# Position bias of layer 0: two kinds of DMA change their issuing engine, and the softmax its step

## The chip, the cores and the metric

The program runs on one core of a Trainium2 chip. The metric is the device time of one execution in microseconds. Three executions of the kernel before took 3286.91, 3290.55 and 3295.93 us, so the median is 3290.55 us. A separate execution was recorded by the hardware profiler.

## What is computed

Four layers are chained; only the first matters here. It is an attention over an image of 32 x 32 positions, with 2 images and 8 heads each, so 16 heads in all. Every head has 1024 queries and 64 keys, whose places are sampled by learned offsets. To every score a bias is added, which a small network of three layers computes for each pair of a query and a key:

```python
pos = grid_q[:, :, None, :] - grid_kv[:, None, :, :]
bias = jnp.sign(pos) * jnp.log1p(jnp.abs(pos))
bias = jax.nn.relu(bias @ cpb_w1 + cpb_b1)          # 2 -> 128
bias = jax.nn.relu(bias @ cpb_w2 + cpb_b2)          # 128 -> 128
bias = (bias @ cpb_w3 + cpb_b3).reshape(b, GROUPS, H * W, Hd * Wd)
sim = jnp.einsum('bhid,bhjd->bhij', qh, kh) + bias
attn = jax.nn.softmax(sim, axis=-1)
out = jnp.einsum('bhij,bhjd->bhid', attn, vh)
```

All arithmetic is in fp32. The bias network over 16 x 1024 x 64 pairs is the bulk of layer 0.

## The kernel before

**Steps.** `layer0` walks through 256 steps `(u, o, half)`: `u` is the head (0 to 15), `o` a group of 8 keys (0 to 7), and `half` one of its two sets of 4 keys. The text writes (4,1) for `o` = 4, `half` = 1. The order on PE, ScalarE (ACT), VectorE (DVE) and GpSimd (POOL) is written out by hand under `manual_schedule`; each engine runs its own list in that order. SyncE (SP) is not in that set; its DMA issues are placed by the framework, and SP runs them one after the other as well.

**A step.** `first_hidden` (called one step ahead) makes the first hidden layer of 4 keys on DVE (line 741), four instructions of 128 x 1024, from a table `tx` (x part) and a row `bank` (y part, line 726). `second_hidden` multiplies by the second weights, one quarter `q` of the 128 outputs at a time: 16 matmuls of line 768 give one tile `hp` in PSUM, of which there are three. ACT takes the ReLU of each quarter from PSUM (line 782; q0 is also multiplied by a sign, lines 785 and 787). In some steps of `u` > 0 (`late`, `early`) DVE takes one quarter instead (lines 777 and 780). The four quarters are then added: q0 into q1 by an accumulating DMA that POOL issues (line 792), q2 into q3 by POOL (line 796), and both sums by POOL in the next step (`join`, line 799). Quarter tiles `h2_0` have two buffers, so a ReLU of q0 needs the DMA of line 792 of two steps before to have landed.

**Folding.** The tile of q3 holds both halves of a group; three such tiles exist (`two_tiles`). `refold` halves its partitions by accumulating DMAs (lines 802, 824, 827), and two copies on SP (line 834, `sum<-h`) gather the rest into one of two tiles `sum` of the head. These copies come two groups after their group, and the tile is free for the group after that. Three `sum` tiles rotate over the heads, so the copies of group 1 into the second `sum` tile of head `u` write where the first `sum` tile of head `u-1` still lies.

**Summed rows.** While head `u` is in its groups 1 to 4, the two `sum` tiles of head `u-1` are finished: ACT multiplies by a sign (line 222), POOL issues two accumulating DMAs (lines 839 and 841, `keys_rows`), and two copies of 64 KB put the result into the tile `rows` (line 845, on SP). The `refolds` list says at which step each piece is issued: the copies of the first tile at the end of step (3,0), those of the second at the end of step (4,0). At (5,0) `attend` is queued: it adds `rows` to the scores and takes the softmax on DVE and ACT, one piece per step (lines 890 to 940).

**Logarithms.** `table` works for two groups at a time. In the steps that prepare odd groups it loads the next 16 keys' logarithms (`lb<-logs`, 512 KB, broadcast to 128 partitions, line 678 through `send`, line 493) into one of two buffers, and puts a POOL instruction right behind it in POOL's order that turns their x part into `tx` (line 681). `send` issues on SP, behind the last gathering copy recorded in `self.gathered`, which lines 831, 834 and 845 set. The load for groups 6 and 7 is thus issued in the step (4,1), behind the row copies of the second `sum` tile in SP's order.

**Other front work.** The offsets and sampled keys of later pairs of heads run as generators, one piece per step (`front`), and yield to `attend` (`after`).

Of the kernel before, what the change touches and what calls it, by code (L numbers as in the profile page):

```python
# [11 lines left out]
F32 = mybir.dt.float32  # L12
# [6 lines left out]
P = 128  # L19
B, C, H, W = 2, 512, 32, 32  # L20
# [3 lines left out]
HF = 512  # L24
# [33 lines left out]
class Net:  # L58
# [40 lines left out]
    def layer0(self):  # L99


        nc, io = self.nc, self.io
        with ExitStack() as ctx:
# [45 lines left out]
            with self.tc.manual_schedule(engines=engines):  # L149
                pairs = [{} for _ in range(BP)]  # L150
# [26 lines left out]
                tables = {}  # L177
# [12 lines left out]
                for i, (u, o, half) in enumerate(quads):  # L190
                    self.half = half
                    if o == 2 and half == 1 and u % 2 == 0 and u // 2 + 1 < BP:
                        nxt = pairs[u // 2 + 1]
                        front += [self.offsets(nxt, u // 2 + 1, ps), self.sampled(nxt, u // 2 + 1, ps)]
                    h1 = ready
                    if i + 1 < len(quads):
                        if quads[i + 1][1:] == (7, 0) and u + 1 < 2 * BP:
                            self.advance(front, lambda: "logs" in pairs[(u + 1) // 2])
                        ready = self.first_hidden(*quads[i + 1], pairs, tables)
                    last_set = u == last and o >= 4  # L200
                    if half == 0:
                        if o == 0:
                            before, sums = sums, []
                        if o % 4 == 0:
                            group = []
                        if i + 2 < len(quads):
                            both = self.two_tiles(f"h2_{u}_{o}3")
                            group.append([both[:, 0, :], both[:, 1, :], both])
                        else:
                            group.append([self.four_rows(f"h2_{u}_{o}{n}3") for n in range(2)])  # L210
                        if o < 2:
                            sums.append(self.four_rows(f"sum{u}_{o}"))
                    self.second_hidden(i, u, o, half, h1, group[-1], i + 1 == len(quads), last_set)
                    if half == 1 and not last_set:
                        end = i + (3 if u == last else 4)
                        self.refolds.append((i + 2, end, end, self.refold(group[-1][2], sums[o % 2], o // 2, u == last)))
                    v = u - 1
                    if half == 1 and o in (1, 2) and 0 <= v < last - 1:
                        z = before[o - 1]
                        if o == 1:  # L220
                            rows = self.soft.tile([P, HF], F32, tag="pt", name=f"rows{v}")
                        nc.scalar.activation(z, z, AF.Copy, scale=self.last_sign)
                        self.refolds.append((i + 2, i + 4, i + 3, self.keys_rows(z, rows, o - 1)))
                    if half == 1 and o == 2 and v >= 0:
                        sims[v] = ps_s.tile([P, HF], F32, tag="sim", name=f"sim{v}")
                        if v == last - 1:
                            self.sum_product(sims[v], self.thrice, True, before)
                        self.advance(front, lambda: "v" in pairs[v // 2])
                        self.keys_queries(v, pairs[v // 2], sims[v], v < last - 1)
                    if v >= 0 and (o, half) == ((5, 0) if v < last - 1 else (2, 1)):  # L230
                        if v == 8:
                            self.advance(after, lambda: False)
                            att = [apool.tile([P, N], F32, tag=f"att{t}", name=f"att{v}_{t}") for t in range(CT)]
                        after.append(self.attend(v, pairs[v // 2], sims[v], att, ps, rows if v < last - 1 else None))
                        if v % 8 == 7:
                            after.append(self.projection(ps, att, ow, v // 8))
                    elif half == 1 and u == last and o == 5:
                        sims[u] = ps_s.tile([P, HF], F32, tag="sim", name=f"sim{u}")
                        self.sum_product(sims[u], self.twice[:, 16:48], True, sums)
                    elif half == 1 and u == last and o == 7:  # L240
                        self.sum_product(sims[u], self.folded[:, 8:40], False, [one[0] for one in group[:2]])
                    self.refold_more(i, True)
                    if not self.step(after):
                        self.step(front)
# [419 lines left out]
    def turn(self, m, bt, ps):  # L664
# [2 lines left out]
            self.nc.tensor.transpose(tr[:, n, :], m["xn"][:, n * P : (n + 1) * P], self.ident)  # L667
        return tr

    def table(self, u, o, pairs, tables):  # L670

        nc = self.nc
        def load(u, c):
            logs = pairs[u // 2]["logs"].rearrange("(a j c i) e -> a c j (i e)", a=2, j=2, c=4)[u % 2, c]
            got = self.lpool.tile([P, 2, 8, 2, W], F32, tag="logs", name=f"lb{u}{c}")
            self.send(got.rearrange("p j i d x -> p j (i d x)"), logs.unsqueeze(0).to_broadcast([P, 2, 16 * W]))
            x = self.tab.tile([P, 2, 8, W], F32, tag="x", name=f"tx{u}{c}")
            with self.behind(self.added):  # L680
                nc.gpsimd.tensor_scalar(  # L681
                    x, got[:, :, :, 0, :], self.col("cpb_w1", 0), self.col("cpb_b1"), ALU.mult, ALU.add
                )
            tables["next"] = got, x

        y = self.bank[:, 0:256].rearrange("p (i x) -> p i x", i=8)
        jj = o % 2
        if u == 0 and o < 2:


            if o == 0:
                tables["x"] = self.tab.tile([P, 2, 8, W], F32, tag="x", name="tx00")
            else:
                load(0, 1)
            mask = self.ident[:, 32 * jj : 32 * jj + 8]
            parts = []
            for d in range(2):
                at = self.fone.tile([P, 8, W], F32, tag=f"first{d}", name=f"first{o}{d}")
                nc.vector.tensor_tensor(
                    at,  # L700
                    pairs[0]["log"][:, d, :].unsqueeze(1).to_broadcast([P, 8, W]),
                    mask.unsqueeze(2).to_broadcast([P, 8, W]),
                    ALU.mult,
                )
                got = self.ps_h.tile([P, 8, W], F32, tag="ps", name=f"lb_ps{o}{d}")
                nc.tensor.matmul(
                    got.rearrange("p k x -> p (k x)"),
                    lhsT=self.all,
                    rhs=at.rearrange("p k x -> p (k x)"),
                    start=True,  # L710
                    stop=True,
                )
                parts.append(got)
            next(self.weights)
            x = tables["x"][:, jj, :, :]
            nc.scalar.activation(x, parts[0], AF.Identity, scale=self.col("cpb_w1", 0), bias=self.col("cpb_b1"))
            nc.vector.tensor_scalar(y, parts[1], self.col("cpb_w1", 1), None, ALU.mult)
            if o == 0:
                next(self.weights)
            return x, y  # L720
        if o % 2 == 0:
            tables["logs"], tables["x"] = tables.pop("next")
        elif u < 2 * BP - 1 or o < 7:

            load(*((u, o // 2 + 1) if o < 7 else (u + 1, 0)))
        nc.vector.tensor_scalar(y, tables["logs"][:, jj, :, 1, :], self.col("cpb_w1", 1), None, ALU.mult)
        return tables["x"][:, jj, :, :], y

    def first_hidden(self, u, o, half, pairs, tables):

        if half == 0:
            tables["xy"] = self.table(u, o, pairs, tables)
        x, y = tables["xy"]
        h1 = [self.hid.tile([P, 2, H, W], F32, tag="h1", name=f"h1_{u}_{o}{half}{r}") for r in range(2)]

# [100 lines left out]
    def keys_rows(self, z, to, jj):  # L836

        nc = self.nc
        nc.gpsimd.dma_start(z[0::2], z[1::2], accum_op=ALU.add)
        yield  # L840
        nc.gpsimd.dma_start(z[0::4], z[2::4], accum_op=ALU.add)
        yield
        for h in range(2):
            at = h * NJ + jj * 32
            self.gathered = nc.sync.dma_start(to[at : at + 32, :], z[0::4, h * HF : (h + 1) * HF])

    def sum_product(self, sim, lhsT, start, zs):

# [1348 lines left out]
```

## Time and profile before

| | |
|---|---|
| median of three executions | 3290.55 us |
| the profiled execution | 3290.0 us, span 3288.3 us, mean granted TensorE clock 0.995 |
| matmuls of line 768 | first at 22.9 us, last at 1966 us |
| PE busy | 3217.4 us, 98% of the span |
| DVE, ACT, POOL busy | 75%, 58%, 72% of the span |
| between 138 and 1853 us: PE, DVE, ACT, POOL busy | 1660, 1375, 1262, 1511 of 1715 us |
| loads of logarithms | 63, all on SP, median 6.3 us from issue to landing |
| copies into `rows` | 56, all on SP, median 2.6 us from issue to landing |

The profile's groups name a line, an engine, an operation and the tiles it writes and reads. A wait is idle time of an engine, put down to the event that ended it last; where that event was long over, another one released the engine. Heads 1 to 14 are the ones with the full pattern; their steps lie between 138 us (first matmul of head 1) and 1853 us (first matmul of head 15).

### The profile page before, as it was taken

To read this page: it belongs to the slowest core of one execution; us is meant where nothing else is said; L and a number is where in the kernel's file an instruction comes from. 1 tells how busy PE (TensorE), PEld (TensorE's weight loads), DVE (VectorE), ACT (ScalarE), POOL (GpSimd) and SP (SyncE) were. 2 spreads that over 40 slices of the span, in tenths; PEclk is the share of its full clock that TensorE was granted. 3 is DMA by queue.
4 is the path that set the end of the run, shared out by engine and by line. 5 is a ranking of instruction groups with operands and counts; after the bars stand their busy time and mean duration, and the time that the engine had idled before them with its cause. 6 is when DMAs were issued, how large, how long until landed. Compare 5 with 4: busy or idle time off the path is not lost.

```text
span 3288.3 us, 58784 instructions
## 1 busy us (share of the span) xinstructions
PE 3217.4 (98%) x23956; PEld 1210.3 (37%) x23956; DVE 2470.8 (75%) x2834; ACT 1905.2 (58%) x1985; POOL 2362.1 (72%) x1664
## 2 busy tenths in 40 slices
PE   9999999999999999999999999999999999999999
PEld 4333233233233323233333224444465533455333
DVE  7888878888878677888877775565565689855897
ACT  7877777777777577777777661111141466213662
POOL 7989888988988779989888974344153458534575
PEclk9999999999999999999999999999999999999999
DMA  6887787787787668787787763111000100000001
GB/s 169 161 173 158 147 174 154 154 169 152 152 163 154 129 136 165 148 172 158 146 171 157 152 151 137 39 44 47 0 1 1 39 1 1 15 1 13 1 1 53
DMA packets 96591, 341.92 MB, mean 104 GB/s; under 512 B 19888, under 2 KB 22064, under 8 KB 79216
## 3 DMA queue, kind: packets, MB, share of 16 engines
q0 software_dynamic: 56224, 244.88, 39.2%
q1 hardware_dynamic: 39072, 91.00, 9.0%
q8 instruction: 193, 3.16, 0.4%
q10 hardware_dynamic: 1008, 2.10, 0.2%
q14 instruction: 94, 0.77, 0.1%
HBM read 67.37 MB, written 4.46 MB: 22 GB/s over the span
## 4 chain that ended last, share of the span: by engine, by line
PE 63%; POOL 16%; DVE 9%; DMA 6%; issue 4%; ACT 1%; SPq 0%; DVEq 0%; POOLq 0%; ACTq 0%
PE hp L768 26%; POOL h L799 7%; PE s L1730 5%; PE o L1759 5%; DMA h<-h 3%; POOL h L796 3%; DVE h L741 3%; POOL h L792 2%; PE qk20P L1505 1%; PE qk30P L1505 1%; PE m_0P L1014 1%; PE m_7P L1014 1%; PE m_5P L1014 1%; PE m_4P L1014 1%; PE m_2P L1014 1%
## 5 line engine op out<-in xcount | busy, mean ns | idle before, releaser
L768 PE MATMUL hp<-h,w2s 128*32 128x512 f32 x16384 | 1816.7, 597 | 53.5 <-ACT h L782 47.9
L782 ACT ACTIVATE h<-hp,magb 128x1024 f32<-128x1024 f32 x950 | 1043.1, 1108 | 470.9 <-PE hp L768 306.5
L741 DVE CUSTOM_DVE_ANT_1 h<-tx,bank 128x1024 f32<-128x1024 f32 (+1 forms) x1028 | 1180.4, 1210 | 161.2 <-PE hp L768 121.7
L768 PEld LDWEIGHTS hp<-h,w2s 128*32 128x32 f32 x16384 | 559.0, 110 | 1276.8 <-issue 1069.1
L799 POOL TENSOR_TENSOR h<-h,h 128x1024 f32<-128x1024 f32 x254 | 750.5, 2955 | 14.0 <-DMA h<-h 11.8
L796 POOL TENSOR_TENSOR h<-h,h 128x1024 f32<-128x1024 f32 x209 | 661.9, 3167 | 5.1 <-ACT h L782 5.1
L792 POOL DMA_DIRECT2D h<-h x227 | 333.8, 1471 | 73.0 <-ACT h L782 64.6
L1734 ACT ACTIVATE e<-s 128x1024 f32<-128x1024 f32 x256 | 261.8, 1024 | 181.0 <-PE s L1730 175.1
L1759 PE MATMUL o<-e,v 64*64 64x512 f32 x2048 | 265.3, 589 | 2.1 <-DVE q L1798 2.1
L1730 PE MATMUL s<-q,k 64*64 64x512 f32 x2048 | 266.0, 591 | 0.0
L787 ACT ACTIVATE h<-h,flip 128x1024 f32<-128x1024 f32 x182 | 209.6, 1152 | 6.0
L1741 POOL TENSOR_TENSOR some<-some,e 128x1024 f32<-128x1024 f32 x64 | 167.6, 2619 | 26.6 <-ACT e L1734 24.1
L1739 POOL TENSOR_TENSOR some<-e,e 128x1024 f32<-128x1024 f32 x32 | 76.0, 2376 | 141.4 <-DVE sum L1748 102.4
L802 POOL DMA_DIRECT2D h<-h x127 | 173.1, 1363 | 6.1 <-issue 4.0
L824 POOL DMA_DIRECT2D h<-h x124 | 168.3, 1358 | 7.6 <-DMA h<-h 5.1
L827 POOL DMA_DIRECT2D h<-h x120 | 148.7, 1239 | 17.0 <-DMA h<-h 16.8
L681 POOL TENSOR_SCALAR tx<-lb,cols 128x512 f32<-128x512 f32 x63 | 78.4, 1245 | 108.9 <-DMA lb<-logs 72.5
L1746 DVE TENSOR_TENSOR sum<-sum,e 128x1024 f32<-128x1024 f32 x64 | 123.9, 1936 | 29.6 <-ACT e L1734 26.9
L984 POOL TENSOR_TENSOR mlp_w<-mlp_w 128x512 f32<-128x512 f32 x16 | 23.5, 1470 | 158.7 <-DMA mlp_w<-in_mlp_w 113.5
L1759 PEld LDWEIGHTS o<-e,v 64*64 64x64 f32 x2048 | 77.9, 133 | 144.9 <-issue 135.1
L1730 PEld LDWEIGHTS s<-q,k 64*64 64x64 f32 x2048 | 76.6, 133 | 133.2 <-issue 117.2
L777 DVE SCALAR_TENSOR_TENSOR h<-hp,under,h 128x1024 f32<-128x1024 f32 x46 | 59.0, 1283 | 79.1 <-ACT h L782 69.4
(595 smaller groups left out, 3583.5 us busy)
## 6 DMA issues: line engine op xcount, KB each, us to landing
h<-h POOLq DMA_DIRECT2D x354, 512.0 KB, 5.8
lb<-logs SPq DMA_DIRECT2D x63, 512.0 KB, 6.3
h<-h POOLq DMA_DIRECT2D x124, 256.0 KB, 4.3
mlp_w<-in_mlp_w SPq DMA_DIRECT2D x16, 1024.0 KB, 4.8
h<-h POOLq DMA_DIRECT2D x120, 128.0 KB, 3.8
sum<-h SPq DMA_DIRECT2D x240, 64.0 KB, 3.4
sum<-sum POOLq DMA_DIRECT2D x28, 256.0 KB, 5.0
x<-in_x SPq DMA_DIRECT2D x8, 512.0 KB, 7.9
```

Source lines behind the costliest of these rows:

```text
L741: self.nc.vector._custom_dve(TENSOR_ADD_SAT, out=h1[r][:, k, cut, :], in0=x[:, 4 * half + 2 * r + k, :].unsqueeze(1).to_broadcast([P, H // ...
L768: nc.tensor.matmul(hp[rows, cut], lhsT=self.l0w2[:, 32 * q : 32 * q + 32], rhs=h1[k][:, cut], start=True, stop=True)
L782: nc.scalar.activation(y, hp, AF.Relu, bias=self.magb[:, q, 0:1])
L787: nc.scalar.activation(y, y, AF.Copy, scale=self.flip)
L792: self.added = pool.dma_start(y, ys[0], accum_op=ALU.add)
L796: self.added = (vec if final else pool).tensor_tensor(y, y, ys[2], ALU.add)
L799: (vec if final else pool).tensor_tensor(z, z, other, ALU.add)
L802: pool.dma_start(one[2][0::2], one[2][1::2], accum_op=ALU.add)
L824: nc.gpsimd.dma_start(both[0::4], both[2::4], accum_op=ALU.add)
L1730: nc.tensor.matmul(s[halves[c], par, :], lhsT=ks[p][rows, at : at + DH], rhs=qs[p][rows, cut], start=True, stop=True)
L1734: nc.scalar.activation(e, s, AF.Exp, scale=DH**-0.5)
L1759: nc.tensor.matmul(o[halves[par], r, :], lhsT=v[n // 2][rows, n % 2, at : at + DH], rhs=e[rows, par, :], start=(n == 0), stop=(n == NB - 1),)
```

## The change

The copies into `rows` are issued by ACT instead of SP, no longer set `self.gathered`, and stand one step later: the first tile's at the end of (3,1), the second's at the end of (4,1). `attend` is queued at (5,1) instead of (5,0). For the groups 2, 4 and 6 (and 2 only from head 1 on) the load of logarithms moves from SP, in the step that prepares an odd group, to ACT, one step earlier: it stands in ACT's order ahead of the ReLUs of (0,0), (2,0) and (4,0). That makes 47 of the 63 loads; the loads for the next head's groups 0 and 1 stay on SP. The POOL instruction that makes `tx` stays at its place in POOL's order. No other instruction is added or removed; the pieces of `front` and `attend` fall into other steps here and there, because one yields to the other.

```diff
-                        self.refolds.append((i + 2, i + 4, i + 3, self.keys_rows(z, rows, o - 1)))
+                        self.refolds.append((i + 2, i + 4, i + 4, self.keys_rows(z, rows, o - 1)))
...
-                    if v >= 0 and (o, half) == ((5, 0) if v < last - 1 else (2, 1)):
+                    if v >= 0 and (o, half) == ((5, 1) if v < last - 1 else (2, 1)):
...
+    def load(self, u, c, pairs, early):
+
+        logs = pairs[u // 2]["logs"].rearrange("(a j c i) e -> a c j (i e)", a=2, j=2, c=4)[u % 2, c]
+        got = self.lpool.tile([P, 2, 8, 2, W], F32, tag="logs", name=f"lb{u}{c}")
+        to, what = got.rearrange("p j i d x -> p j (i d x)"), logs.unsqueeze(0).to_broadcast([P, 2, 16 * W])
+        if early:
+            self.nc.scalar.dma_start(to, what)
+        else:
+            self.send(to, what)
+        return got
...
-        def load(u, c):
-            logs = pairs[u // 2]["logs"].rearrange("(a j c i) e -> a c j (i e)", a=2, j=2, c=4)[u % 2, c]
-            got = self.lpool.tile([P, 2, 8, 2, W], F32, tag="logs", name=f"lb{u}{c}")
-            self.send(got.rearrange("p j i d x -> p j (i d x)"), logs.unsqueeze(0).to_broadcast([P, 2, 16 * W]))
+        def spread(u, c):
+            got = tables["loaded"] if "loaded" in tables else self.load(u, c, pairs, False)
+            tables.pop("loaded", None)
...
         if half == 0:
             tables["xy"] = self.table(u, o, pairs, tables)
+        elif o % 2 == 0 and o < 6 and (u > 0 or o > 0):
+            tables["loaded"] = self.load(u, o // 2 + 1, pairs, True)
...
-            self.gathered = nc.sync.dma_start(to[at : at + 32, :], z[0::4, h * HF : (h + 1) * HF])
+            nc.scalar.dma_start(to[at : at + 32, :], z[0::4, h * HF : (h + 1) * HF])
```

More of the change, by code (lines that the diff above doesn't have):

```diff
@@ L693, in table @@
             else:
-                load(0, 1)
+                spread(0, 1)
             mask = self.ident[:, 32 * jj : 32 * jj + 8]
@@ L723, in table @@
         elif u < 2 * BP - 1 or o < 7:
-            load(*((u, o // 2 + 1) if o < 7 else (u + 1, 0)))
+            spread(*((u, o // 2 + 1) if o < 7 else (u + 1, 0)))
         nc.vector.tensor_scalar(y, tables["logs"][:, jj, :, 1, :], self.col("cpb_w1", 1), None, ALU.mult)
```

## The prediction

> **What bounds the kernel now.** I read the busy times first, then the windows of heads 1 to 14, their waits, and last the timelines of single heads around the two places that the diff touches.
>
> ```profile
> PE 3217.4 (98%) x23956; PEld 1210.3 (37%) x23956; DVE 2470.8 (75%) x2834; ACT 1905.2 (58%) x1985; POOL 2362.1 (72%) x1664
> ```
>
> PE is the bound. A change to DMA issues can give only what PE stands still, and what its clock loses after that. In the windows view (window, length, busy us and instructions of PE, PEld, DVE, ACT, POOL, granted clock, DMA share, GB/s):
>
> ```profile
> 138.00:1853.00 1715.00, 1660.43 (x14987) 526.25 (x14988) 1375.39 (x1491) 1262.45 (x1232) 1511.44 (x1083) 0.99 0.77 156
> 340.00:350.00 10.00, 6.59 (x40) 1.64 (x44) 7.58 (x8) 5.58 (x6) 10.00 (x8) 0.66 0.70 134
> ```
>
> PE stands still for 1715 - 1660.4 = 54.6 us there. The second window follows a stall of 3.98 us in PE's timeline: the clock is 0.66, so matmuls are slower too. Undisturbed, 128 matmuls of L768 take 13.87 us in PE's timeline, and a step of 64 takes 6.87 (one boundary in two costs 0.13). The 224 steps of heads 1 to 14 need 224 x 6.87 = 1539, PE's other work there is 79.7, so 1715 - 1539 - 80 = 96 us are excess, idle and slow matmuls together. I took each step's length in PE's timeline less 6.87 and less the other work in it: 34 us lie at (3,1) to (5,0), 63.5 at (5,1) to (7,1), and nothing to speak of elsewhere. Who ends the waits in this window (us, times, longest):
>
> ```profile
> ACT h L782 <- DMA h<-h: 90.3, 38, 6.8
> POOL tx L681 <- DMA lb<-logs: 66.1, 10, 8.6
> ...
> PE hp L768 <- ACT h L782: 47.9, 35, 5.9
> ...
> ACT h L782 <- DMA sum<-h: 40.7, 24, 4.5
> DVE sampling L604 <- DMA at<-spots: 36.0, 4, 10.5
> ...
> ACT h L782 <- DMA sum<-sum: 22.6, 5, 8.7
> POOL tx L681 <- DVE bank L897: 21.9, 3, 7.5
> ...
> POOL tx L681 <- DVE bank L903: 14.5, 2, 7.4
> ```
>
> **Stall B**, at (5,1) and after. The timelines of head 4 (start, us, engine, line), of SP, POOL, ACT and PE:
>
> ```profile
> 571.25 1.56 SPq L845 DMA_DIRECT2D rows<-sum  x2
> 572.86 0.58 SPq L493 DMA_DIRECT2D lb<-logs  x1
> ```
> ```profile
> 578.46 0.77 POOL L681 TENSOR_SCALAR tx<-lb,cols 128x512 f32<-128x512 f32 x1 [7.39 <-DVE bank L897]
> 579.18 0.86 POOL L792 DMA_DIRECT2D h<-h  x1
> ```
> ```profile
> 583.64 1.11 ACT L782 ACTIVATE h<-hp,magb 128x1024 f32<-128x1024 f32 x1 [5.32 <-DMA h<-h]
> ```
> ```profile
> 584.81 7.67 PE L768 MATMUL hp<-h,w2s 128*32 128x512 f32 x56 [2.48 <-ACT h L782]
> ```
>
> The load waits behind the row copies, POOL waits 7.39 us for the load (the named bank instruction was long done), the accumulating DMA behind `tx` is late, the ReLU of q0 waits 5.32 us for its buffer, and PE loses 2.48. POOL's wait is in all of heads 1 to 14, 5.2 to 8.6 us each, 102.5 us in sum over the three rows for `tx` above.
>
> **Stall A**, at (4,0). The gathering copies of group 1 into the second `sum` tile wait until the row copies have read that buffer; ACT's q3 waits for those copies, through its own buffer. In head 3, ACT and PE:
>
> ```profile
> 447.41 1.11 ACT L782 ACTIVATE h<-hp,magb 128x1024 f32<-128x1024 f32 x1 [8.73 <-DMA sum<-sum]
> ```
> ```profile
> 448.58 3.65 PE L768 MATMUL hp<-h,w2s 128*32 128x512 f32 x20 [5.90 <-ACT h L782]
> ```
>
> In both places PE loses ACT's wait less about 2.8 us (5.32 to 2.48, 8.73 to 5.90); shorter waits of ACT cost nothing.
>
> **What the Trainium skill says.** "DMA: Bandwidth & Descriptors", section "Anatomy of one DMA — SWDGE (gpsimd) path": a DMA engine does not wait on semaphores, the wait is on the issuing sequencer before dispatch. The trace agrees: the load leaves SP at 572.86, directly behind the two row copies. So whatever queue takes the row copies takes their wait as well. Same page, "Issuing engines are not separate DMA queues": DMAs of different engines run on the same 16 DMA engines. Here these are 0.77 busy, so a load issued by ACT still competes with SP's copies; the trace of before has no such case. "TensorE: Matmul & The Clock Gate", "Part 1: The HAM clock gate": after about 3.4 us idle the clock falls to half. The window at 340 agrees: 0.66 as a mean over 10 us.
>
> **The change, part by part.**
>
> *Loads on ACT, one group sooner.* At (4,0) the load is ahead of the ReLUs and about 14 us, two steps, sooner; it lands 6.3 us (median of its DMA row) after issue, so POOL's 7 us wait is covered. Removed: stall B at (5,1) to (7,1): 43.4 us in the even heads (7.7, 6.1, 5.8, 5.3, 3.7, 5.6, 9.2), 8.2 + 4.7 in heads 9 and 11, 1.2 in head 1: **-57**. The rest of the 63.5, 1.5 each in heads 3, 5, 7 and 13, follows DVE's softmax and stays. POOL is still late: at (4,1) it is 5.2 to 11.9 us behind, and PE begins to lose at about 9.2. Without the wait this lag falls by 0 to 2 us by (6,1); its worst heads lose a little: **+5**, bounds 0 and 12.
>
> *Issues on ACT.* 47 loads and 56 copies are 103 issues. ACT's own DMA issues at the program's start took 0.33 to 0.47 us, SP's row copies 0.49 to 1.13: 103 x 0.45 = 46 to 103 x 0.59 = 61 us, over 1715 in which ACT is busy 1262. ACT's 450 idle us hide it, **0**; without that cover, if each issue pushed a ReLU that PE waits for, +46 to +61. The load's own waits on ACT (its buffer's last readers) ended two steps earlier.
>
> *Row copies on ACT.* They wait in ACT's order for the accumulating DMAs (L839, L841). In the trace of before those of the first tile land between 3.9 us before and 3.0 us after ACT's last ReLU of (3,1), where the copies now stand; those of the second between 4.4 before and 0.7 after that of (4,1). So ACT waits 3.0 at most, and only about 0.2 above the 2.8 that cost PE nothing: **0**. Behind a waiting copy stand the ReLUs of (4,0) and (5,0), and PE behind these.
>
> *Stall A.* Where the landing was early, in even heads, the copies now leave up to 3.9 us later (u4 3.7, u6 2.6, u8 3.9, u10 2.2, u12 and u14 1.3), and so do the gathering copies of group 1, and ACT's q3 of (4,0). Its start may lie 9.5 us behind that of the step before PE loses; heads 8 and 14 would pass this. The load issued directly behind the copies takes DMA bandwidth from them, 0 to 2 us. Together **+6**, bounds 0 and 20 (20: all seven even heads lose 2.9).
>
> *Odd heads.* Stall A costs 7.6, 5.8, 8.5, 2.3, 6.1 us in heads 3, 5, 7, 11, 13. A POOL that does not stall by 7 us issues L839 and L841 sooner in relation to its steps, and DVE's wait at L604 (36.0 us in 4 heads) shrinks by 0.3 to 2.8 as `at<-spots` no longer stands behind row copies on SP: **-10** of 30, bounds 0 and -25.
>
> *Softmax one step later.* Its DVE parts are unchanged (the first about 3.3 us: 0.69, 0.72, 0.69, 0.80, 0.18, 0.24), in a step later that has DVE at 1375 of 1715: **0**. If one of them meets the front's work in a step where DVE is full, 1 to 2 us in some heads; that is inside the bounds.
>
> Sum: -57 + 5 + 6 - 10 = **-56**. The profiled execution took 3290.0 us, the median is 3290.55, so either way: **3234 us**. With the better bounds (-57, 0, 0, -25) it is -82, 3208; with the worse ones (-57, +12, +20, 0) -25, 3265.
>
> **Rivals.**
>
> *The wait moves to stall A (0.22).* The rows are later everywhere, and every head loses at (4,0) what it gained at (5,1). For it: only 2.8 us of slack, and even heads are close. Against: odd heads' landings are after ACT's ReLU, so nothing is added there. Seven more heads losing 4 us: -56 + 28 = -28, 3262; range 3252 to 3281.
>
> *Both stalls vanish (0.15).* With POOL early, all of stall A goes but 6 of 34: -57 - 28 = -85, about 3206.
>
> *POOL becomes the bound (0.05).* It is 1511 of 1715 busy, 93% after a gain of 90. If it can't catch up its lag of 8 us, the load was a mask: the wait goes and POOL comes to the same step as late. Against: its wait was 7 us after a lag of 8, beyond a tolerance of 9.2. Within 10 us of before, 3281 to 3300.
>
> *Slower: ACT is blocked by its own copies (0.07).* There are 28 places, two in each of 14 heads. PE loses ACT's wait less 2.8. It decides from a mean wait of 2.8 + 56 / 28 = 4.8 us; at 6 us it is 28 x 3.2 = 90, 3290 - 56 + 90 = 3324. For it: a loop, in which a late ACT makes POOL late, and POOL the landing. Against: landings in the trace of before are at most 3.0 us late.
>
> That the change does not do what it says I exclude: in the order of the built kernel the loads stand ahead of (4,0)'s ReLUs with no late wait, and PE, DVE and POOL keep their main order.
>
> **How the numbers follow.** The likeliest, 3234 with its own range 3215 to 3252, has 0.51; the moved stall 0.22, both stalls gone 0.15, POOL 0.05, ACT blocked 0.07. The range is 3206 to 3272: it leaves out half of the best case (0.07), the last two (0.12) and the upper end of the moved stall (0.02), 0.2 in all. About 0.3%, 10 us, is what a measurement can tell from no change: faster 0.88, same 0.05, slower 0.07.
>
> **What would show it.** Right: `tx` on POOL waits under 10 us in sum, where it was 102; ACT's wait for `h<-h` falls from 90 to below 40; PE's idle time in heads 1 to 14 from 54.6 to 15 to 20; no ACT wait over 3 us ahead of a row copy; at (4,0) the wait for `sum<-h` stays near 41 and heads 8 and 14 lose a little more. Wrong if ACT shows long waits at L845 (the slower rival), if waits for the `sum` copies grow in all heads (moved), or if POOL, never idle at (4,1), is still late at L792 of (5,0).

## The result, and the profile after

The changed kernel took 3255.79 us (median of four executions, 3249.9 to 3257.2) where the kernel before, run again beside it, took 3291.86. The ratio is 0.9888, with a 95% interval of 0.9869 to 0.9907: 36 us faster. The profiled execution took 3257.2 us (span 3255.5) against 3290.0, so 33 us less. 3234 was forecast, 56 us less, with a range of 3206 to 3272: the direction and the range held, the gain was about two thirds of the forecast one.

The page's busy times, and the window of heads 1 to 14, which now begin at 138.4 and end at 1820.2 us (window, length, busy us and instructions of PE, PEld, DVE, ACT, POOL, granted clock, DMA share, GB/s):

```profile
PE 3205.5 (98%) x23956; PEld 1216.4 (37%) x23956; DVE 2475.8 (76%) x2834; ACT 1906.6 (59%) x1985; POOL 2361.8 (73%) x1664
```
```profile
138.40:1820.20 1681.80, 1646.50 (x14978) 531.12 (x14980) 1378.95 (x1489) 1263.42 (x1231) 1512.00 (x1083) 0.99 0.79 159
```

Heads 1 to 14 take 1681.8 us instead of 1714.8; the whole difference is here. PE stands still for 1681.8 - 1646.5 = 35.3 us instead of 54.6; 15 to 20 was forecast. The step lengths, less 6.87 us and less PE's other work in them (the excess), tell where:

| excess, heads 1 to 14 (us) | before | after | difference |
|---|---|---|---|
| (5,1) to (7,1), stall B | 63.6 | 5.2 | -58.4 |
| (3,1) to (5,0), stall A | 33.5 | 55.0 | +21.5 |
| of this, even heads | 2.9 | 17.2 | +14.3 |
| of this, odd heads | 30.6 | 37.7 | +7.1 |
| (0,0) to (2,1) | -1.0 | 3.9 | +4.9 |

So stall B is gone as forecast, and about a third of the gain is lost again one group earlier. The view of waits of the same window (us, times, longest) says the same:

```profile
ACT h L794 <- DMA sum<-h: 59.4, 17, 6.0
DVE sampling L604 <- DMA at<-spots: 39.2, 5, 9.9
...
PE hp L780 <- ACT h L794: 32.8, 18, 6.4
...
ACT h L794 <- DMA sum<-sum: 13.0, 4, 8.4
...
ACT h L794 <- DMA h<-h: 2.6, 2, 1.8
```

ACT's wait for `h<-h`, behind which stall B stood, fell from 90.3 to 2.6 us, and the 102.5 us that POOL waited for `tx` have no line any more. ACT's waits put down to `sum<-h` and `sum<-sum` rose from 63.3 to 72.4 us in the whole window. By steps the change is larger: at (3,1) to (5,0), where the copies of group 1 stand, they rose from 35 to 60 us, while the 17 us at (5,1) to (7,1) went to nothing.

Head 4, which had no stall at (4,0) before, shows it. Before, the timelines of SP and ACT had no wait for the two gathering copies:

```profile
553.74 1.48 SPq L845 DMA_DIRECT2D rows<-sum  x2
556.94 1.84 SPq L834 DMA_DIRECT2D sum<-h  x2
```
```profile
554.05 3.29 ACT L782 ACTIVATE h<-hp,magb 128x1024 f32<-128x1024 f32 x3
```

After, the timelines of ACT with its DMA queue, of SP, of POOL and of PE:

```profile
554.35 1.13 ACTq L857 DMA_DIRECT2D rows<-sum  x2
...
557.57 0.36 ACTq L676 DMA_DIRECT2D lb<-logs  x1
...
566.94 2.12 ACT L794 ACTIVATE h<-hp,magb 128x1024 f32<-128x1024 f32 x2 [4.46 <-DMA sum<-h]
```
```profile
559.12 1.13 SPq L846 DMA_DIRECT2D sum<-h  x2
```
```profile
571.03 1.43 POOL L691 TENSOR_SCALAR tx<-lb,cols 128x512 f32<-128x512 f32 x1
```
```profile
568.11 17.37 PE L780 MATMUL hp<-h,w2s 128*32 128x512 f32 x160 [2.25 <-ACT h L794]
```

The load leaves 1.55 us ahead of the two gathering copies; these need 7.7 us from issue to the last landing in this head, where they needed 3.9 before; ACT's q3 waits 4.46 us and PE 2.25. `tx` no longer waits. The chain behind this, as means over heads 1 to 14 from the records' issues and landings:

| us | landing of L841's DMA, to the start of (4,0) | landing to issue of row copies | row copies, to the last landing | gathering copies, to the last landing | ACT's q3 after the start of (4,0) |
|---|---|---|---|---|---|
| before | -0.01 | 0.15 | 3.94 | 4.40 | 9.4 |
| after | -0.70 | 0.54 | 4.95 | 6.71 | 11.8 |

(L841 is L853 in the numbering of the changed kernel.) The largest new piece is 2.3 us in the gathering copies.

### The profile page after: what moved, and what is told of

It reads as the page before. It is cut to its first block, busy times and chain, and to the rows that moved or that the text cites. A ratio compares the mean times of both kernels' runs of the same rounds, so it can differ in the third digit from the quotient of the medians.

```text
span 3255.5 us, 58764 instructions
## 1 busy us (share of the span) xinstructions
PE 3205.5 (98%) x23956; PEld 1216.4 (37%) x23956; DVE 2475.8 (76%) x2834; ACT 1906.6 (59%) x1985; POOL 2361.8 (73%) x1664
## 3 DMA queue, kind: packets, MB, share of 16 engines
HBM read 67.37 MB, written 4.46 MB: 22 GB/s over the span
## 4 chain that ended last, share of the span: by engine, by line
PE 62%; POOL 17%; DMA 7%; DVE 7%; issue 4%; ACT 2%; ACTq 0%; SPq 0%; POOLq 0%; DVEq 0%
PE hp L780 25%; POOL h L811 7%; PE s L1742 5%; PE o L1771 5%; POOL h L808 5%; DMA h<-h 3%; POOL h L804 2%; DMA sum<-h 2%; ACT h L794 2%; PE qk30P L1517 1%; PE qk20P L1517 1%; PE m_7P L1026 1%; PE m_5P L1026 1%; PE m_4P L1026 1%; PE m_2P L1026 1%
## 5 line engine op out<-in xcount | busy, mean ns | idle before, releaser
L811 POOL TENSOR_TENSOR h<-h,h 128x1024 f32<-128x1024 f32 x254 | 739.2, 2910 | 15.9 <-DMA h<-h 13.8
L808 POOL TENSOR_TENSOR h<-h,h 128x1024 f32<-128x1024 f32 x209 | 656.8, 3142 | 6.1 <-ACT h L794 6.1
L804 POOL DMA_DIRECT2D h<-h x227 | 295.3, 1301 | 139.5 <-ACT h L794 138.2
L836 POOL DMA_DIRECT2D h<-h x124 | 174.3, 1405 | 16.6 <-DMA h<-h 9.6
L814 POOL DMA_DIRECT2D h<-h x127 | 162.9, 1283 | 6.0 <-issue 3.9
L839 POOL DMA_DIRECT2D h<-h x120 | 137.3, 1144 | 5.9 <-DMA h<-h 5.4
L1092 ACT ACTIVATE mh<-mh,cols 128x512 f32<-128x512 f32 x64 | 46.1, 721 | 124.3 <-DVE mh L1110 64.3
```

The source lines that it names most:

```text
L804: self.added = pool.dma_start(y, ys[0], accum_op=ALU.add)
L808: self.added = (vec if final else pool).tensor_tensor(y, y, ys[2], ALU.add)
L811: (vec if final else pool).tensor_tensor(z, z, other, ALU.add)
L836: nc.gpsimd.dma_start(both[0::4], both[2::4], accum_op=ALU.add)
```

## The experiments

Theory 1: the early load of 512 KB shares the DMA engines with the small copies of the chain at (4,0) and makes these slower. Theory 2, the rival of the order: the row copies now stand behind a ReLU on ACT, leave later, and the rest follows. The kernel before, run beside these kernels, took 3291.7 to 3292.4 us.

### Row copies back on SyncE

```diff
-self.refolds.append((i + 2, i + 4, i + 4, self.keys_rows(z, rows, o - 1)))
+self.refolds.append((i + 2, i + 4, i + 3, self.keys_rows(z, rows, o - 1)))
...
-            nc.scalar.dma_start(to[at : at + 32, :], z[0::4, h * HF : (h + 1) * HF])
+            self.gathered = nc.sync.dma_start(to[at : at + 32, :], z[0::4, h * HF : (h + 1) * HF])
```

> The changed kernel with its row copies back on SyncE and one step sooner, as in the kernel before; early loads on ScalarE and the later softmax stay. Theory 2 (order): the excess at (3,1) to (5,0) falls back to about 34 us: 3234 to 3238. Theory 1 (contention): the load still leaves beside these copies; only the 0.4 us per head between landing and issue are gained: excess 48 to 55, 3248 to 3256.

3263.4 us (3260.1 to 3264.0), ratio to before 0.9912 (0.9896 to 0.9929): no gain over the changed kernel, rather a loss, and above the ranges of both theories. The excess at (3,1) to (5,0) is 53.4 us, as theory 1 had it. The row copies leave 0.20 us after the landing, and the gathering copies still take 6.22. So theory 2 doesn't explain the sum.

By heads it explains a part. Four kernels have the softmax at (5,1) and differ in the other two parts; the excess at (3,1) to (5,0) splits in them about as follows (us in sum over these heads; the first two kernels have their own sections below):

| | row copies | early loads | even heads 2 to 12 | odd heads |
|---|---|---|---|---|
| only the softmax moved | on SP | no | 1 | 29 |
| only the row copies moved | on ACT | no | 2 to 3 | 13 |
| row copies back on SP | on SP | yes | 2 | 43 |
| changed kernel | on ACT | yes | 13 | 38 |

So in these even heads neither the early loads nor the later row copies cost much alone; together they do. The landings fit: on average over all even heads the gathering copies land 8.4 us after the start of (4,0) with the row copies back on SP, 8.7 with the row copies moved alone, and 11.2 in the changed kernel, and by the prediction's reading ACT's q3 may start about 9.5 us after that start before PE loses. In the odd heads the early loads cost by themselves. With the softmax at (5,0), the even heads 2 to 12 lose about 8 us by the row copies alone and 16 with the loads too.

### The load one step later, at (4,1)

```diff
-        elif o % 2 == 0 and o < 6 and (u > 0 or o > 0):
+        elif o % 2 == 0 and o < 4 and (u > 0 or o > 0):
...
         if half == 0:
+            if o == 5:
+                tables["loaded"] = self.load(u, 3, pairs, True)
```

(`first_hidden` is called one step ahead, so `o == 5`, `half == 0` is ACT's step (4,1).)

> The changed kernel, but the load for groups 6 and 7 goes out at the head of ScalarE's step (4,1), one step later than in the changed kernel. Theory 1 (contention): the load leaves when most gathering copies of group 1 have landed, the excess at (3,1) to (5,0) falls to 35-42 us; the load lands about 7 us into the step, where GpSimd needs it at 8, so a wait of 0 to 1 us per head: 3236 to 3246. Theory 2 (order): 3252 to 3260.

3237.6 us (3234.6 to 3240.1), ratio 0.9832 (0.9815 to 0.9848). The gathering copies take 4.71 us, and the excess at (3,1) to (5,0) is 30.3. POOL waits 0.1 to 3.9 us for `tx` in six heads, 13.2 us in sum. 18 us come back by moving one load by one step. Theory 1 holds here.

### The load one step sooner, at (3,1)

```diff
-        elif o % 2 == 0 and o < 6 and (u > 0 or o > 0):
+        elif o % 2 == 0 and o < 4 and (u > 0 or o > 0):
...
         if half == 0:
+            if o == 4:
+                early = self.load(u, 3, pairs, True)
             tables["xy"] = self.table(u, o, pairs, tables)
+            if o == 4:
+                tables["loaded"] = early
```

> The changed kernel, but the load of logarithms for groups 6 and 7 goes out at the head of ScalarE's step (3,1) instead of (4,0), so that it lands before the first row copies leave; the two other early loads stay. Theory 1 (DMA contention): in the changed kernel the 512 KB load leaves directly behind the first row copies, and rows and gathering copies of group 1 share the DMA engines with it; from landing of the accumulating DMA to the last gathering copy it is 12.4 us on average where it was 8.6. Then here it is 8.6 to 9.6, the excess at (3,1) to (5,0) falls from 55 to 35-40 us, and the time is 3236 to 3242 (after: 3255.8). Theory 2 (order: the row copies now stand behind a ReLU in ScalarE's order): the same rows wait as in the changed kernel, so 3252 to 3258.

3260.3 us (3256.6 to 3262.3), ratio 0.9904 (0.9888 to 0.9921): the expectation failed. The gathering copies are fast again (3.77 us), but the chain ahead of them is late: the DMA of L841 takes 5.58 us from issue to landing instead of 4.09 in the changed kernel and lands 1.28 us after the start of (4,0) instead of 0.70 before it, and the row copies take 5.53. The excess at (3,1) to (5,0) falls only to 44.4, and the other places gain 7.3 us of excess. My expectation had counted the copies of the chain that the load leaves, and not the transfers of the same chain that it meets one step sooner. ACT is held up as well: in 13 of the 14 heads it stands idle for 1.6 to 6.4 us at the head of (4,0), right behind the issue of the row copies.

### Only the row copies moved

The kernel before with L845 on ACT one step later and the softmax at (5,1); no early loads.

```diff
-self.refolds.append((i + 2, i + 4, i + 3, self.keys_rows(z, rows, o - 1)))
+self.refolds.append((i + 2, i + 4, i + 4, self.keys_rows(z, rows, o - 1)))
...
-                    if v >= 0 and (o, half) == ((5, 0) if v < last - 1 else (2, 1)):
+                    if v >= 0 and (o, half) == ((5, 1) if v < last - 1 else (2, 1)):
...
-            self.gathered = nc.sync.dma_start(to[at : at + 32, :], z[0::4, h * HF : (h + 1) * HF])
+            nc.scalar.dma_start(to[at : at + 32, :], z[0::4, h * HF : (h + 1) * HF])
```

> The kernel before with only the row copies moved to ScalarE (and the later softmax); all loads stay on SyncE in their old steps. The load for groups 6 and 7 no longer stands behind row copies, only behind the gathering copies of group 1. Theory 1: it leaves some 5 us sooner than before and beside the end of those copies, lands in time for GpSimd, so the wait of 102 us is gone without the early load, and the excess at (4,0) is between that of before (34) and after (55): 3236 to 3252. If the earlier place of the load is needed for the gain, GpSimd still waits 3 us or more per head and the time is 3265 to 3285.

3225.3 us (3224.0 to 3231.7), ratio 0.9801 (0.9785 to 0.9818): 30 us faster than the whole change, better than the expectation. The load for groups 6 and 7 is still the one on SP; with the row copies gone from SP it leaves 5.8 us after the start of (4,0) (mean over the heads) where it left at 17.9, directly behind the two gathering copies. In head 4, SP and then POOL:

```profile
548.97 1.26 SPq L834 DMA_DIRECT2D sum<-h  x2
550.32 0.53 SPq L493 DMA_DIRECT2D lb<-logs  x1
```
```profile
558.62 2.00 POOL L681 TENSOR_SCALAR tx<-lb,cols 128x512 f32<-128x512 f32 x1
```

POOL reaches `tx` 8 us later and does not wait; over heads 1 to 14 it waits 5.6 us in sum, once 2.6. The gathering copies take 4.28 us, and the excess is 18.5 us at (3,1) to (5,0), less than before. DVE's wait for `at<-spots`, 36.0 us before, is 20.8. So the early loads were not needed for the gain at (5,1).

This edit changes the engine of the copies and their step at once. One kernel was not run: the copies still on SP, but at the end of (4,1). In the order of the program the load is issued earlier in that same step, so they might no longer be ahead of it there either. So it is not shown that they have to leave SP.

### The load as an addition

To measure the contention alone, the kernel of the last section got one more load: ACT loads the same logarithms into the same buffer at the head of (4,0), and SP's load fills it again with the same values. SP's load has to wait for the first one to land.

```diff
+        elif o == 4 and u > 0:
+            tables["twice"] = self.load(u, o // 2 + 1, pairs, True)
...
-    def load(self, u, c, pairs, early):
+    def load(self, u, c, pairs, early, got=None):
...
-        got = self.lpool.tile([P, 2, 8, 2, W], F32, tag="logs", name=f"lb{u}{c}")
+        got = got or self.lpool.tile([P, 2, 8, 2, W], F32, tag="logs", name=f"lb{u}{c}")
...
-            got = tables["loaded"] if "loaded" in tables else self.load(u, c, pairs, False)
+            got = tables["loaded"] if "loaded" in tables else self.load(u, c, pairs, False, tables.pop("twice", None))
```

> The kernel with only the row copies on ScalarE (3225.3) plus one more load: the logarithms of groups 6 and 7 are also loaded by ScalarE at the head of (4,0), where the changed kernel has it, into the same buffer that SyncE's load fills again a little later. Nothing waits for the extra load but that second one. Contention alone: the excess at (3,1) to (5,0) rises from 18.5 to 40-55 us, as in the changed kernel, and the time to 3245-3262; from landing of the accumulating DMA to the last gathering copy 11.5 to 13 us instead of 9.7. If contention is not the cause (but, say, the place of the load for GpSimd, or of the two other early loads), 3224 to 3233: only 14 issues of 0.5 us on ScalarE are added.

3251.3 us (3249.6 to 3259.3), ratio 0.9883 (0.9866 to 0.9900): 26 us slower than without it. The gathering copies take 6.71 us instead of 4.28, as in the changed kernel, and the excess at (3,1) to (5,0) is 47.9 instead of 18.5. ACT's and PE's timelines of head 4, without the extra load:

```profile
553.90 2.12 ACT L782 ACTIVATE h<-hp,magb 128x1024 f32<-128x1024 f32 x2 [1.58 <-DMA sum<-h]
```
```profile
548.46 14.10 PE L768 MATMUL hp<-h,w2s 128*32 128x512 f32 x128
```

With it, the timelines of ACT, SP and PE:

```profile
552.02 0.36 ACTq L676 DMA_DIRECT2D lb<-logs  x1
...
562.14 2.12 ACT L794 ACTIVATE h<-hp,magb 128x1024 f32<-128x1024 f32 x2 [5.21 <-DMA sum<-h]
```
```profile
553.58 1.12 SPq L846 DMA_DIRECT2D sum<-h  x2
559.08 0.36 SPq L493 DMA_DIRECT2D lb<-logs  x1
```
```profile
563.31 3.23 PE L780 MATMUL hp<-h,w2s 128*32 128x512 f32 x16 [3.01 <-ACT h L794]
```

Up to the load the two are alike, but for a shift of 4.6 us. Then ACT's wait is 5.21 instead of 1.58 us, and PE, which ran through, loses 3.01. Windows over those copies (549 to 554 without, 553.6 to 562 with the load) show a DMA share of 0.88 and 1.03:

```profile
549.00:554.00 5.00, 5.00 (x52) 1.98 (x47) 4.96 (x6) 3.39 (x5) 4.93 (x7) 1.00 0.88 195
```
```profile
553.60:562.00 8.40, 6.70 (x64) 2.45 (x55) 8.23 (x9) 3.30 (x4) 6.62 (x8) 1.00 1.03 205
```

So one load at this place, ahead of the copies, brings 29 us of the 36 that lie between the excess of the row copies alone (18.5) and of the changed kernel (55.0). A load beside the copies is in both kernels of this section; SP's own leaves 1.35 us behind them in head 4, and over heads 1 to 14 the copies take no longer than before (4.28 against 4.40). It is the place ahead of them that costs. How the DMA engines share their time between the two was not looked at.

### The other two early loads

The changed kernel with the load for groups 6 and 7 back on SP (the condition reads `o < 4`); and the same with only the one for group 2 early (`o == 0 and u > 0`).

```diff
-        elif o % 2 == 0 and o < 6 and (u > 0 or o > 0):
+        elif o % 2 == 0 and o < 4 and (u > 0 or o > 0):
```

> The changed kernel, but the load for groups 6 and 7 is back on SyncE in its old step; the loads for groups 2 and 4 stay early on ScalarE, the row copies on ScalarE. If the loss lies in the load for groups 6 and 7 alone, this equals the kernel with only the row copies moved: 3222 to 3230. If each early load costs, 3234 to 3246.

> Row copies on ScalarE, softmax at (5,1), and of the early loads only that for group 2, at (0,0) of heads 1 to 15. With the loads for groups 2 and 4 both early it was 3239.6, with neither 3225.3. If the load at (2,0) does the damage, 3224 to 3230; if both share it, 3230 to 3236; if the one at (0,0), 3236 to 3241.

With both early 3239.6 us (3238.0 to 3241.9), ratio 0.9838 (0.9822 to 0.9855); with the first alone 3230.8 (3229.5 to 3236.1), ratio 0.9818 (0.9802 to 0.9834). So from 3225.3 us on, the three early loads cost 5.5, 8.8 and 16.2 us. Those of the first two again show at (3,1) to (5,0): the excess is 23.0 and 34.1. In the trace with both, POOL comes to (2,1) 2.8 and 2.7 us later in heads 5 and 7 than without. Which transfer of that stretch they slow down was not separated.

### The softmax

Four kernels set the softmax against the other parts (the row copies on ACT stand one step later in all of them): the changed kernel with it back at (5,0), the row copies on ACT alone with it at (5,0), the early loads alone with it at (5,0), and the kernel before with nothing but the later softmax. The edit is the same in each, in one direction or the other:

```diff
-                    if v >= 0 and (o, half) == ((5, 0) if v < last - 1 else (2, 1)):
+                    if v >= 0 and (o, half) == ((5, 1) if v < last - 1 else (2, 1)):
```

> The changed kernel with the softmax back at (5,0). With only the row copies moved, the later softmax was worth 3248.5 - 3225.3 = 23 us. If this worth is independent of the loads, 3272 to 3282. If it came only where the other stalls had been removed, 3255 to 3264.

> Only the row copies on ScalarE at (3,1) and (4,1), the softmax queued at (5,0) as before. The rows of the second tile land some 3 us into (5,0), and VectorE's first softmax instruction stands in that step. If the later softmax is a necessary part of the change, VectorE waits 2 to 5 us per head and PE loses a part of it: 3235 to 3265. If VectorE reaches that instruction after the rows have landed, 3222 to 3229, no different from 3225.3.

> The early loads on ScalarE alone; row copies on SyncE and softmax at (5,0) as before. GpSimd's wait at (4,1) is gone (-57), the load contends at (4,0) (+20 on the excess of 33.5), and the softmax costs up to 20 of what was gained: 3262 to 3285. If the load contends only together with row copies on ScalarE, the excess at (3,1) to (5,0) stays at 34 and the time is 3232 to 3245.

> The kernel before with only the softmax queued at (5,1) instead of (5,0). The stall at (5,1) to (7,1), 63.5 us, comes from the late load and stays; if VectorE's softmax work was hidden behind it, 3287 to 3295, no different from before. If the later softmax has a worth of its own, as the 23 us beside the row copies, 3265 to 3280.

| median, us | softmax at (5,0) | softmax at (5,1) |
|---|---|---|
| nothing else changed | 3291.9 | 3289.9 |
| row copies on ACT | 3248.5 | 3225.3 |
| early loads on ACT | 3263.5 | 3263.4 |
| both | 3257.2 | 3255.8 |

The ratio of the softmax alone is 0.9993 (0.9985 to 1.0002); the row copies alone have 0.9868 (0.9852 to 0.9885), the loads alone 0.9916 (0.9900 to 0.9933), both without the later softmax 0.9898 (0.9882 to 0.9915). The later softmax is worth 23 us beside the row copies, and nothing clear of the spread of the runs elsewhere. With the row copies on ACT and the softmax at (5,0), DVE reaches it before the second rows have landed. From the view of waits:

```profile
DVE sim L890 <- DMA rows<-sum: 10.7, 4, 3.4
...
DVE sim L890 <- issue: 3.8, 2, 2.4
```

The excess at (5,1) to (7,1) is 25.5 us there and 8.6 with the later softmax, which has no such wait; at (3,1) to (5,0) it is 26.0 and 18.5, and at (0,0) to (2,1) -1.0 and 4.6. These 14.5 us of waiting are a part of the 23; the rest lies in how DVE's pieces fall into the steps, and wasn't separated. In the changed kernel the later softmax also lowers (5,1) to (7,1), from 17.0 to 5.2 us, but the excess at (3,1) to (5,0) is 55.0 with it and 39.9 without, and that at (0,0) to (2,1) is some 5 us higher too. Why the earlier place profits from the earlier softmax was not settled.

### A faster version

The kernel with only the row copies moved, with the accumulating DMAs of the rows and the copies all one step sooner:

```diff
-self.refolds.append((i + 2, i + 4, i + 4, self.keys_rows(z, rows, o - 1)))
+self.refolds.append((i + 1, i + 3, i + 3, self.keys_rows(z, rows, o - 1)))
```

> The row copies on ScalarE, and the accumulating DMAs of the rows and those copies all one step sooner than in the kernel with only the row copies moved (copies at the ends of (3,0) and (4,0)); loads as before, softmax at (5,1). If the chain from those DMAs to the gathering copies of group 1 is all that is left of the stall at (4,0), its 18.5 us fall to 2-8: 3208 to 3216. If GpSimd's late issue sets it, the chain starts no sooner: 3220 to 3230.

3220.1 us (3219.1 to 3222.5), ratio 0.9782 (0.9765 to 0.9798), the fastest of all. The chain starts 6 us sooner (the landing is 7.05 us before (4,0)), ACT's q3 comes 4 us after the gathering copies have landed, and its waits for them are gone from the view of waits. Yet the excess at (3,1) to (5,0) is 20.4, not 2 to 8; it fell only at (5,1) to (7,1), from 8.6 to 2.4. The time lies in the other range, 3220 to 3230, but not for its reason, a chain that starts no sooner. So that chain was not what was left: heads 3, 5, 9 and 11 still lose 3.0 to 3.9 us each at (3,1) to (5,0), without a wait for `sum` and with one of 0.6 us for `at`. The cause is open.

## Why the prediction was right, and where it was wrong

**The sum: right in direction and range, in part by luck.** The forecast terms were -52 at stall B and -4 at stall A; measured are -58.4 and +21.5, and +4.9 at (0,0) to (2,1), which had no term. The range held because it was wide enough for an error of 25 us at stall A, of which stall B gave 6 back.

**Stall B: right in place and chain; the size needed a part that was put at nothing.** -57 for the loads was forecast; with the +5 for POOL's lag it is -52, and -58.4 was measured. With the softmax at (5,0), though, the loads and row copies leave 17.0 us there, so they bring -46.6, and the later softmax the other -11.8. Some 5 us of this lie in heads 3, 5, 7 and 13, where the prediction itself put 1.5 us each down to the softmax and took them to stay. Whether POOL's lag cost something can't be read from this. Nor does the gain need the early loads: it comes as well from moving the row copies. The prediction had seen that the load stands behind them; it costed the parts of the edit together and never asked what the move of the row copies alone would do. It would have been 3225, not 3256.

**Stall A in even heads: the mechanism was right, its size was off.** +6 was taken, with bounds 0 and 20; it is +14.3. The step that failed is "the load issued directly behind the copies takes DMA bandwidth from them, 0 to 2 us". Over heads 1 to 14 the gathering copies alone became 2.3 us slower on average, which is above that range, and with them the row copies 1.0, of which 0.7 is there without any early load too (4.66 us). The other piece, row copies up to 3.9 us later, was overestimated: in the even heads 4 to 14 they leave 0.3 to 1.4 us later, and in head 2 they leave sooner. But it is needed: with the row copies back on SP, the even heads 2 to 12 lose 2 us in sum instead of 13. That the two add up to pass the 9.5 us was the prediction's own argument, and it holds in more heads than the two it named.

**Odd heads: wrong sign.** -10 was taken, +7.1 measured. With the row copies alone the odd heads' excess does fall, from 30.6 to 13.1, and the DMA of L841 lands in them 1.0 us before the start of (4,0) instead of 0.9 after it. This fits the reasons given, a POOL that does not stall and a sooner `at<-spots`; which of them brings it was not separated. But the early loads take it back. `at<-spots` takes 6.7 us (median) to land in the changed kernel where it took 5.2, and DVE's wait for it is 39.2 us, not less than 36.0. The prediction had charged contention only to the copies directly behind the load, in even heads; the runs show it in odd heads too, and for L841's DMA when the load stands at (3,1).

**Row copies on ACT: nearly free, though not within the bound.** The prediction bounded ACT's wait by 3.0 us. In the changed kernel ACT stands idle up to 5.4 us ahead of its ReLUs at the head of (4,0) (head 3), 12.4 us in four such waits, and head 3 loses 2.0 us in that step. So the bound failed and the slower rival's mechanism exists, but it is far from that rival's 4.8 us on average.

**Softmax: 0 was right only as a sum.** In the changed kernel it takes about 12 us off stall B and adds about 15 at stall A and 5 at (0,0) to (2,1). That its worth is 23 us beside the row copies alone had no place in the sum.

**The rivals.** The measured time, 3255.8, lies in the range of "the wait moves to stall A" (3252 to 3281, chance 0.22), not in the likeliest's own range. Its place was right: the price in its text, some 4 us in seven more heads, is 28 us against the 21.5 measured. Its reason, later row copies, was half right: in even heads they are one of two causes, but with the copies back on SP the whole excess stays at 53.4. POOL did not become the bound: its waits for `tx` are gone, and stall B with them. That both stalls vanish comes nearest to true in the kernel with the row copies alone, where 18.5 and 8.6 us are left.

## What to carry to other kernels

When a load that is waited for stands behind other transfers on its queue, first take these from ahead of it and see when it leaves; sending it from another engine as early as its buffer allows is a second change with a price of its own. In this kernel the large transfer did best just behind the small ones on the path that sets the end, not ahead of them: one step made 18 us, one load of 512 KB in each head 26. Undo each part of a change alone, since the parts of this one were worth -43 (row copies), -28 (early loads) and -2 us (softmax, within the spread of the runs) alone and -36 together. And look at the groups of heads apart: with the later softmax, two parts that cost the even heads 2 to 12 1 to 2 us each cost them 11 together.

## What the runs showed of the hardware that was not expected

What a 512 KB load costs two 64 KB copies depends on where it stands beside them. The means over heads 1 to 14: issued 1.5 to 4.9 us ahead of them, it made them take 6.71 us instead of 4.28 (kernel with the extra load, against the one without); 1.6 us behind them on average (row copies alone) they took 4.28, 4.9 us behind (load at (4,1)) 4.71, 13.7 us behind (kernel before) 4.40, and 14 us ahead (load at (3,1)) 3.77. The kernels differ in other transfers too, so only the first pair is a comparison of the load's place alone. In head 4 the DMA share was about 1 where they were slow and 0.88 where they were not, while the extra load itself took about as long as ever (6.5 us where 6.3 is the median of before). The load at (3,1) met other transfers instead: a 128 KB accumulating DMA went from 4.09 to 5.58 us.

At a mean DMA share of 0.77 to 0.79 over heads 1 to 14, hiding a transfer was not free: the mean says nothing of the microseconds in which a short copy has to land.
